# A graph-attention layer on one core: the fill work between attention steps is cut into smaller pieces

## The chip, the cores and the metric

The kernel runs on one core of a Trainium2 chip. The metric is the device time of one execution in microseconds (us). TensorE (PE), VectorE (DVE), ScalarE (ACT), GpSimd (POOL) and SyncE (SP) have instruction streams of their own [...].

## The reference

Eight frames `f` of 2048 nodes with 256 channels go through one masked attention layer with eight heads of 32 channels, a two-layer network, and three layer norms:

```python
qkv = jnp.einsum('fnc,ck->fnk', x, w_qkv)            # x: 8 x 2048 x 256
scores = jnp.einsum('fnhd,fmhd->fhnm', q, k) / sqrt(32)
scores = jnp.where(adj > 0, scores, -1e9)            # adj: 2048 x 2048, sparse
attn = softmax(scores, axis=-1)
t = jnp.einsum('fhnm,fmhd->fnhd', attn, v)
a = layernorm(x + t, ln1_g, ln1_b)
h = relu(a @ w1 + b1)
b = layernorm(a + h @ w2 + b2, ln2_g, ln2_b)
out = layernorm(x + b)
```

## The kernel before, in words

**Items.** The attention is a list of 1024 items `(f, qc, g, mb)`: frame, block of 512 query rows, group of four heads, block of 128 key rows. Sixteen items (`mb` 0 to 15) make a group, two groups make a block `(f, qc)`, four blocks make a frame. For one item:

- `scores` (L168): four matmuls (L176) write four heads of transposed scores into two PSUM pairs (of three, `ps_s`, used in turn). DVE adds the mask while it moves each pair to a tile `p` in SBUF (L179, two instructions), and ACT takes the exponential of the whole tile in place (L181). `p` has ten buffers.
- `values` (L185): four matmuls (L193) add `v` times `p` into a PSUM bank that the group owns for its sixteen items. After the last, ACT copies it to `oT` (L197).
- `add_up` (L205): the softmax denominators need the sum of the sixteen `p` tiles. Six items of `POOLED` are added to the group's first tile by GpSimd (L212). Items of the two `MOVED` chains are added to the chain's first tile by an accumulating DMA, which GpSimd issues (L209). The last item is left alone.

The main loop (L358) writes the order out by hand. At step `t` it calls `advance(t, banks)`, then `scores` of item `t + 2`, then `values` and `add_up` of item `t`. Each engine executes its part of that order.

**Fill work.** Everything else is a Python generator in the list `fill`, and `advance` emits pieces of it between items. A generator yields `k` when it is to go on `k` items later, `BANK` when its next piece needs a PSUM bank, and `TURNED` when it needs the tile `turned`, which one generator at a time may hold. `advance` hands out one bank in a step (two in odd steps of the "hurried" stretches: the last group of `qc` 3 and the first half group of a frame). All these banks are one and the same PSUM tile: of the two `ps_x` tiles one belongs to the running group and the other is for fill work, with one buffer. The generators are:

- `denominator` (L237), four items after each group: sixteen matmuls of the four remaining `p` tiles with a matrix of ones (L245) as one piece, an ACT copy (L247), four transposes (L252), the reciprocal (L257).
- `tail` (L263), one for each block, two items after the denominators of its second group: transposes of `oT` (L272), the scaling by the reciprocals (L273), the residual `x` added by an accumulating DMA (L277), `norm`, two transposes into `turned` (L287), two GpSimd operations over 128x1024 (L290, L291), the two layers (L297, L307), `norm`, two more GpSimd operations (L312, L313), the second residual (L314), `norm`, and the store (L317).
- `norm` (L215): for each of four row blocks bn_stats and bn_aggr on DVE (L219, L220), two row blocks to a step; four small GpSimd operations (L224 to L228); two items later four ACT scalings (L231) in one step.
- `project` (L127), four in a frame for the next frame: transposes, then `kT`, `qT` and `v` in six pieces with one bank each (L150, L159) and an ACT copy each.
- `mask_ahead`, in frame 0 alone: turns the adjacency matrix into the mask tiles.

New denominators and tails go to the front of `fill`, the rest to its end.

Of the kernel before, what the change touches and what calls it, by code (L numbers as in the profile page):

```python
# [18 lines left out]
P = 128  # L19
H = 8  # L20
D = 32
CH = 512
# [3 lines left out]

SUM_MIN = 1e-25
SUM_MAX = 1e19
BANK, TURNED = -1, -2

MASKED = -57344.0

# [21 lines left out]
def fast_path(ctx, tc, cst, x, adj, out, RS):  # L54
    nc = tc.nc
    F, N, C = x.shape
    NCK, TPC, MB = N // CH, CH // P, N // P
# [16 lines left out]
    ctx.enter_context(tc.manual_schedule())  # L74

    ident, identb, wqkv, w1s, w2s = cst["ident"], cst["identb"], cst["wqkv"], cst["w1s"], cst["w2s"]
    state = {"pair": 0, "side": None, "turn": 0, "turned": False}

    def score_pair():
        i = state["pair"]  # L80
# [85 lines left out]
    PT, O, OT, RC = {}, {}, {}, {}  # L166
# [16 lines left out]
    LAST = MB - 1  # L183
# [14 lines left out]

    POOLED = (0, 3, 5, 8, 10, 12, 14)
    MOVED = ((1, 4, 7, 11), (2, 6, 9, 13))
    SUM = 4

    def add_up(item):  # L205
# [9 lines left out]
    def norm(t):  # L215
        mv = small.tile([P, TPC, nc.vector.BN_AGGR_DIM], F32, name="mv")
        for j in range(TPC):
            st = small.tile([P, nc.vector.BN_STATS_DIM], F32, name="st")
            nc.vector.bn_stats(st, t[:, j, :])  # L219
            nc.vector.bn_aggr(mv[:, j, :], st)  # L220
            if j % 2:
                yield 1
        rs = small.tile([P, TPC], F32, name="rs")
        nc.gpsimd.tensor_scalar(rs, mv[:, :, 1], EPS, 1.0, op0=ALU.add, op1=ALU.mult)  # L224
        nc.gpsimd.tensor_tensor(rs, rs, cst["mhalf"], ALU.pow)  # L225
        nb = small.tile([P, TPC], F32, name="nb")
        nc.gpsimd.tensor_tensor(nb, mv[:, :, 0], rs, ALU.mult)  # L227
        nc.gpsimd.tensor_scalar(nb, nb, -1.0, 1.0, op0=ALU.mult, op1=ALU.mult)  # L228
        yield 2
        for j in range(TPC):  # L230
            nc.scalar.activation(t[:, j, :], t[:, j, :], AF.Identity, bias=nb[:, j:j + 1], scale=rs[:, j:j + 1])  # L231
        yield 1

    def rows(v):
        return v[:, None, :].to_broadcast([P, TPC, C])

    def denominator(f, qc, g):  # L237
        grp = (f, qc, g)
        terms = [PT.pop((f, qc, g, LAST))] + [PT.pop((f, qc, g, chain[0])) for chain in MOVED + (POOLED,)]
        yield BANK  # L240
        ps = bank()
        for n, term in enumerate(terms):
            for h in range(4):
                r = D * h
                nc.tensor.matmul(ps[r:r + D, :], cst["ones"], term[:, h, :], start=(n == 0), stop=(n == 3))  # L245
        dT = op.tile([P, CH], F32, name="dT")
        nc.scalar.copy(dT, ps)  # L247
        yield 1
        yield BANK
        ps = bank()  # L250
        for j in range(TPC):
            nc.tensor.transpose(ps[:, j * P:(j + 1) * P], dT[:, j * P:(j + 1) * P], ident)  # L252
        if g == 0:
            RC[f, qc] = op.tile([P, TPC, H], F32, name="rc")
        rc = RC[f, qc]
        den = ps.rearrange("p (j c) -> p j c", c=P)[:, :, ::D]
        nc.vector.reciprocal(rc[:, :, 4 * g:4 * g + 4], den)  # L257
        nc.vector.tensor_tensor(RS[:, 0], RS[:, 0], den, ALU.add)
        nc.vector.tensor_tensor(RS[:, 1], RS[:, 1], den, ALU.min)
        if g == 1:  # L260
            start(items.index((f, qc, g, LAST)) + SUM + 2, tail(f, qc), urgent=True)

    def tail(f, qc):  # L263
        rc = RC.pop((f, qc))
        xin = x[f, qc * CH:(qc + 1) * CH, :].rearrange("(j p) c -> p j c", p=P)
        y = yp.tile([P, TPC, C], F32, name="y")
        for gg in range(2):
            oT = OT.pop((f, qc, gg))
            yield BANK
            ps = bank()  # L270
            for j in range(TPC):
                nc.tensor.transpose(ps[:, j * P:(j + 1) * P], oT[:, j * P:(j + 1) * P], ident)  # L272
            nc.vector.tensor_tensor(y[:, :, gg * P:(gg + 1) * P].rearrange("p j (h d) -> p j h d", d=D),  # L273
                                    ps.rearrange("p (j h d) -> p j h d", h=4, d=D),
                                    rc[:, :, 4 * gg:4 * gg + 4, None].to_broadcast([P, TPC, 4, D]), ALU.mult)
        yield 1
        nc.gpsimd.dma_start(y, xin, accum_op=ALU.add)  # L277
        yield 5
        yield from norm(y)
        yield TURNED  # L280
        state["turned"] = True
        yT = work.tile([P, 2, CH], F32, name="turned")
        for a in range(2):
            yield BANK
            ps = bank()
            for j in range(TPC):
                nc.tensor.transpose(ps[:, j * P:(j + 1) * P], y[:, j, a * P:(a + 1) * P], ident)  # L287
            nc.scalar.activation(yT[:, a, :], ps, AF.Identity, bias=cst["be1c"][:, a:a + 1], scale=cst["g1c"][:, a:a + 1])  # L288
        yield 1
        nc.gpsimd.tensor_tensor(y, y, rows(cst["g1r"]), ALU.mult)  # L290
        nc.gpsimd.tensor_tensor(y, y, rows(cst["be1b2r"]), ALU.add)  # L291
        hT = work.tile([P, 2, CH], F32, name="hT")
        for d in range(2):
            yield BANK
            ps = bank()
            for a in range(2):
                nc.tensor.matmul(ps, w1s[:, a, d * P:(d + 1) * P], yT[:, a, :], start=(a == 0), stop=(a == 1))  # L297
            nc.scalar.activation(hT[:, d, :], ps, AF.Relu, bias=cst["b1s"][:, d:d + 1], scale=1.0)  # L298
        state["turned"] = False
        yield 1  # L300
        z = y
        for jj in range(0, TPC, 2):
            yield BANK
            ps = bank()
            for j in range(jj, jj + 2):
                for d in range(2):
                    nc.tensor.matmul(ps[:, (j - jj) * C:(j - jj + 1) * C], hT[:, d, j * P:(j + 1) * P], w2s[:, d, :],  # L307
                                     start=(d == 0), stop=(d == 1))
            nc.vector.tensor_tensor(z[:, jj:jj + 2, :], ps.rearrange("p (b c) -> p b c", c=C), z[:, jj:jj + 2, :], ALU.add)  # L309
        yield 1  # L310
        yield from norm(z)
        nc.gpsimd.tensor_tensor(z, z, rows(cst["g2r"]), ALU.mult)  # L312
        nc.gpsimd.tensor_tensor(z, z, rows(cst["be2r"]), ALU.add)  # L313
        nc.gpsimd.dma_start(z, xin, accum_op=ALU.add)  # L314
        yield 7
        yield from norm(z)
        nc.sync.dma_start(out[f, qc * CH:(qc + 1) * CH, :].rearrange("(j p) c -> p j c", p=P), z)  # L317


    fill = []  # L320

    def start(t, gen, urgent=False):
        fill.insert(0 if urgent else len(fill), [t, gen, 1])

    def advance(t, banks):
        for e in list(fill):
            while e[0] <= t:
                if e[2] == BANK:  # L330
                    if not banks:
                        break
                    banks -= 1
                elif e[2] == TURNED and state["turned"]:
                    break
                e[2] = next(e[1], None)
                if e[2] is None:
                    fill.remove(e)
                    break
                if e[2] > 0:  # L340
                    e[0] = t + e[2]
# [5 lines left out]
    items = [(f, qc, g, mb) for f in range(F) for qc in range(NCK) for g in range(2) for mb in range(MB)]  # L347
# [10 lines left out]
    for t, (f, qc, g, mb) in enumerate(items):  # L358
        if mb == 0 and t:
            state["side"] = 1 - state["side"]  # L360
        if f == 0 and g == 0 and mb == 0 and qc + 1 < NCK:
            start(t, mask_ahead(qc + 1))
        if g == 1 and mb == 0 and (f or qc == NCK - 1) and (f + 1 < F or qc + 1 < NCK):
            load_mask(f + (qc + 1) // NCK, (qc + 1) % NCK)

        if f + 1 < F and (qc, g, mb) in AHEAD:
            start(t, project(f + 1, AHEAD.index((qc, g, mb))))
        if mb:
            hurry = (g, qc) == (1, NCK - 1) or (f and g == qc == 0 and mb < MB // 2)
            advance(t, 2 if hurry and mb % 2 else 1)  # L370
        if t + LEAD < len(items):
            nf, _, ng, nmb = items[t + LEAD]
            t0 = t
            while (nf, nmb // TPC, 1) not in V:
                advance(t0, 1)
                t0 += 1
            scores(items[t + LEAD])
        values(items[t])
        add_up(items[t])
        if mb == LAST:  # L380
            start(t + SUM, denominator(f, qc, g), urgent=True)
    t = len(items)
    while fill:
        t += 1
        advance(t, 1)
# [236 lines left out]
```

## Time and profile before

| | before |
|---|---|
| time, median of 3 | 4048.52 us (4035.02 to 4049.99) |
| span of the profiled execution | 4037.3 us |
| PE busy | 3291.4 us, 82% |
| DVE busy | 2732.3 us, 68% |
| POOL busy | 2621.6 us, 65% |
| ACT busy | 2440.2 us, 60% |
| granted TensorE clock | 0.961 |

The busy shares are means over stretches with different limits: items with no fill work, items with a matmul piece ahead of them, items with norm work. The chain that ended last, which the page lists, covers only the end of the program from 3989.90 us on. To see the limits, the timeline has to be read item by item; the start of each group of eight L176 records (two records to each of four matmuls) marks an item.

### The profile page before, as it was taken

How to read it: one execution, taken by the hardware profiler on the slowest of the kernel's cores; microseconds unless marked ns; L12 is line 12 of the kernel's file. 1: busy time of each engine (PE TensorE's matmuls, PEld its weight loads, DVE VectorE, ACT ScalarE, POOL GpSimd, SP SyncE). 2: the span in 40 equal slices, each digit the busy share in tenths (PEclk: the TensorE clock that was granted, in tenths of full speed). 3: DMA queues.
4: the chain of work that ended last, by engine and by line, in shares of the span. 5: the costliest groups of instructions: out<-in, count | busy, mean ns of one | idle time of the engine just before them, and what ended most of it. 6: DMA issues, size and time to landing. Idle time of an engine off the chain costs nothing. (4 is left out here: it accounts for less than half of the span.)

```text
span 4037.3 us, 53723 instructions
## 1 busy us (share of the span) xinstructions
PE 3291.4 (82%) x22020; PEld 1044.4 (26%) x22020; DVE 2732.3 (68%) x3175; ACT 2440.2 (60%) x1953; POOL 2621.6 (65%) x1355
## 2 busy tenths in 40 slices
PE   7776988888888888888888887888878888888883
PEld 4221332222322223222222222222222222322221
DVE  3766746777477765777667775687756877477772
ACT  4655655666466654666656665566655666566662
POOL 1565656767467765776657766577656777477774
PEclk9988999999999999999999999999999999999996
DMA  4666646667366654677556656476555677367662
GB/s 141 156 142 140 148 95 128 139 145 152 68 146 148 140 128 81 145 148 151 122 112 133 140 126 145 101 153 144 115 128 114 143 148 155 73 141 146 135 137 58
DMA packets 138797, 525.60 MB, mean 130 GB/s; under 512 B 10160, under 2 KB 76848, under 8 KB 85296
## 3 DMA queue, kind: packets, MB, share of 16 engines
q0 software_dynamic: 89088, 436.24, 54.7%
q1 hardware_dynamic: 47104, 83.89, 6.0%
q8 instruction: 174, 2.85, 0.3%
q10 hardware_dynamic: 2352, 1.97, 0.2%
q14 instruction: 79, 0.65, 0.0%
HBM read 98.44 MB, written 20.97 MB: 30 GB/s over the span
## 5 line engine op out<-in xcount | busy, mean ns | idle before, releaser
L179 DVE TENSOR_TENSOR p<-s,mask 128x1024 f32<-128x1024 f32 x2048 | 2410.4, 1219 | 1083.8 <-PE s L176 902.5
L181 ACT ACTIVATE p<-p 128x2048 f32<-128x2048 f32 x1024 | 1952.3, 1910 | 1353.1 <-DVE p L179 1061.1
L212 POOL TENSOR_TENSOR p<-p 128x2048 f32<-128x2048 f32 x384 | 1790.3, 4663 | 931.2 <-ACT p L181 912.3
L176 PE MATMUL s<-qT,kT 32*128 32x512 f32 x8192 | 1212.2, 662 | 354.4 <-DVE p L179 353.5
L193 PE MATMUL x<-p,v 128*32 128x512 f32 x8192 | 1118.1, 618 | 21.4 <-ACT p L181 21.2
L176 PEld LDWEIGHTS s<-qT,kT 32*128 32x128 f32 x8192 | 329.7, 188 | 1010.9 <-DVE p L179 879.4
L209 POOL DMA_DIRECT2D p<-p x384 | 371.8, 979 | 145.7 <-ACT p L181 101.8
L193 PEld LDWEIGHTS x<-p,v 128*32 128x32 f32 x8192 | 162.9, 109 | 834.8 <-issue 528.3
L150 PE MATMUL x<-turned,wqkv 128*128 128x512 f32 x480 | 244.5, 634 | 75.9 <-ACT kT L152 44.2
L245 PE MATMUL x<-p,ones 128*32 128x512 f32 x2048 | 236.3, 602 | 18.9 <-DMA p<-p 8.9
L231 ACT ACTIVATE y<-y,nb,rs 128x256 f32<-128x256 f32 x384 | 197.8, 585 | 40.4 <-POOL nb L228 40.4
L219 DVE BATCH_NORM_STATS2 st<-y 128x6 f32<-128x256 f32 x384 | 155.9, 406 | 23.3 <-DMA y<-in_x_dram 23.3
L297 PE MATMUL x<-turned,w1s 128*128 128x512 f32 x256 | 130.4, 633 | 31.2 <-ACT turned L288 27.1
L159 PE MATMUL x<-wqkv,turned 128*128 128x128 f32 x896 | 124.9, 297 | 34.1 <-ACT qT L152 20.2
L150 PEld LDWEIGHTS x<-turned,wqkv 128*128 128x128 f32 x480 | 84.4, 194 | 239.5 <-issue 94.4
L312 POOL TENSOR_TENSOR y<-y,g2r 128x1024 f32<-128x1024 f32 x32 | 78.1, 2442 | 101.8 <-ACT y L231 101.8
L159 PEld LDWEIGHTS x<-wqkv,turned 128*128 128x128 f32 x896 | 113.5, 206 | 77.2 <-ACT qT L152 38.6
L307 PE MATMUL x<-w2s,hT 128*128 128x256 f32 x512 | 127.6, 392 | 4.0 <-ACT oT L197 1.5
L290 POOL TENSOR_TENSOR y<-y,g1r 128x1024 f32<-128x1024 f32 x32 | 75.7, 2367 | 60.0 <-issue 57.3
L245 PEld LDWEIGHTS x<-p,ones 128*32 128x32 f32 x2048 | 64.0, 111 | 186.2 <-issue 137.2
L307 PEld LDWEIGHTS x<-w2s,hT 128*128 128x128 f32 x512 | 92.0, 189 | 68.8 <-issue 33.3
L287 PE MATMUL x<-ident,y 128*128 128x128 f32 x256 | 53.9, 318 | 62.5 <-ACT y L231 24.4
(67 smaller groups left out, 1366.4 us busy)
## 6 DMA issues: line engine op xcount, KB each, us to landing
p<-p POOLq DMA_DIRECT2D x384, 1024.0 KB, 8.8
y<-in_x_dram POOLq DMA_DIRECT2D x64, 512.0 KB, 6.6
mask<-md SPq DMA_DIRECT2D x28, 1024.0 KB, 14.2
in<-in_x_dram SPq DMA_DIRECT2D x32, 512.0 KB, 13.1
in<-in_adj_dram SPq DMA_DIRECT2D x32, 512.0 KB, 6.4
out_dram<-y SPq DMA_DIRECT2D x32, 512.0 KB, 9.1
md<-mask SPq DMA_DIRECT2D x4, 1024.0 KB, 6.4
wqkv<-in_L_gnn_w_qkv_dram ACTq DMA_DIRECT2D x1, 768.0 KB, 5.9
```

The costliest lines, as they stand in the source:

```text
L150: nc.tensor.matmul(ps, wqkv[:, a, k0 + g * P:k0 + (g + 1) * P], xT[:, a, :], start=(a == 0), stop=(a == 1))
L159: nc.tensor.matmul(ps[:, j * P:(j + 1) * P], xT[:, a, j * P:(j + 1) * P], wqkv[:, a, 2 * C + g * P:2 * C + (g + 1) * P], start=(a == 0), s ...
L176: nc.tensor.matmul(ps2[half][:, j, :], KT[f, mb // TPC, g][r:r + D, (mb % TPC) * P:(mb % TPC + 1) * P], QT[f, qc][r:r + D, g, :], start=Tr ...
L179: nc.vector.tensor_tensor(pt[:, 2 * half:2 * half + 2, :], ps, MK[f, qc][:, mb, None, :].to_broadcast([P, 2, CH]), ALU.add)
L181: nc.scalar.activation(pt, pt, AF.Exp, scale=1.0 / math.sqrt(D))
L193: nc.tensor.matmul(O[grp][r:r + D, :], V[f, mb // TPC, g][:, mb % TPC, r:r + D], PT[item][:, h, :], start=(mb == 0), stop=(mb == LAST))
L209: nc.gpsimd.dma_start(PT[f, qc, g, chain[0]], PT.pop(item), accum_op=ALU.add)
L212: nc.gpsimd.tensor_tensor(first, first, PT.pop(item), ALU.add)
L219: nc.vector.bn_stats(st, t[:, j, :])
L231: nc.scalar.activation(t[:, j, :], t[:, j, :], AF.Identity, bias=nb[:, j:j + 1], scale=rs[:, j:j + 1])
L245: nc.tensor.matmul(ps[r:r + D, :], cst["ones"], term[:, h, :], start=(n == 0), stop=(n == 3))
L307: nc.tensor.matmul(ps[:, (j - jj) * C:(j - jj + 1) * C], hT[:, d, j * P:(j + 1) * P], w2s[:, d, :], start=(d == 0), stop=(d == 1))
```

## The change

It cuts the fill work finer and changes its order.

- `norm` takes one row block to a step in the statistics and in the ACT scalings. Two pairs of GpSimd operations in `tail` are put in separate steps, and so is the issue of the second residual DMA.
- `POOLED` and `MOVED` are laid out anew over the group; the item left alone is 14 and no longer the last.
- The products with ones are emitted in two halves, each after a `BANK`; both write the same bank.
- In `tail` the rows of a block are dealt to the partitions as `(p j)` in place of `(j p)`, so that each partition's four rows are 4 KB in one piece in memory. The transposes of `dT` and `oT` then take every fourth column.
- `fill` is sorted by rank: denominators, then tails, then the rest, each by age. At most two tails run at a time (`ROOM`).

```diff
-    POOLED = (0, 3, 5, 8, 10, 12, 14)
-    MOVED = ((1, 4, 7, 11), (2, 6, 9, 13))
+    POOLED = (0, 3, 6, 8, 11, 13, 15)
+    MOVED = ((1, 4, 7, 10), (2, 5, 9, 12))
+    ALONE = 14
...
             nc.vector.bn_aggr(mv[:, j, :], st)
-            if j % 2:
-                yield 1
+            yield 1
...
             nc.scalar.activation(t[:, j, :], t[:, j, :], AF.Identity, bias=nb[:, j:j + 1], scale=rs[:, j:j + 1])
-        yield 1
+            yield 1
...
         for n, term in enumerate(terms):
+            if n == 2:
+                yield BANK
             for h in range(4):
...
-            nc.tensor.transpose(ps[:, j * P:(j + 1) * P], dT[:, j * P:(j + 1) * P], ident)
+            nc.tensor.transpose(ps[:, j * P:(j + 1) * P], dT[:, j::TPC], ident)
...
-            start(items.index((f, qc, g, LAST)) + SUM + 2, tail(f, qc), urgent=True)
+            start(items.index((f, qc, g, LAST)) + SUM + 2, tail(f, qc), 1)
...
     def tail(f, qc):
+        yield ROOM
+        state["tails"] += 1
...
-        xin = x[f, qc * CH:(qc + 1) * CH, :].rearrange("(j p) c -> p j c", p=P)
+        xin = x[f, qc * CH:(qc + 1) * CH, :].rearrange("(p j) c -> p j c", p=P)
...
-                nc.tensor.transpose(ps[:, j * P:(j + 1) * P], oT[:, j * P:(j + 1) * P], ident)
+                nc.tensor.transpose(ps[:, j * P:(j + 1) * P], oT[:, j::TPC], ident)
...
         nc.gpsimd.tensor_tensor(y, y, rows(cst["g1r"]), ALU.mult)
+        yield 1
         nc.gpsimd.tensor_tensor(y, y, rows(cst["be1b2r"]), ALU.add)
...
         nc.gpsimd.tensor_tensor(z, z, rows(cst["g2r"]), ALU.mult)
+        yield 1
         nc.gpsimd.tensor_tensor(z, z, rows(cst["be2r"]), ALU.add)
+        yield 1
         nc.gpsimd.dma_start(z, xin, accum_op=ALU.add)
...
-    def start(t, gen, urgent=False):
-        fill.insert(0 if urgent else len(fill), [t, gen, 1])
+    def start(t, gen, rank=2):
+        fill.append([t, gen, 1, rank])
+        fill.sort(key=lambda e: e[3])
...
-                elif e[2] == TURNED and state["turned"]:
+                elif e[2] == TURNED and state["turned"] or e[2] == ROOM and state["tails"] == 2:
                     break
...
-            start(t + SUM, denominator(f, qc, g), urgent=True)
+            start(t + SUM, denominator(f, qc, g), 0)
```

More of the change, by code (lines that the diff above doesn't have):

```diff
@@ L28 @@
 SUM_MAX = 1e19
-BANK, TURNED = -1, -2
+BANK, TURNED, ROOM = -1, -2, -3
 MASKED = -57344.0
@@ L76, in fast_path @@
     ident, identb, wqkv, w1s, w2s = cst["ident"], cst["identb"], cst["wqkv"], cst["w1s"], cst["w2s"]
-    state = {"pair": 0, "side": None, "turn": 0, "turned": False}
+    state = {"pair": 0, "side": None, "turn": 0, "turned": False, "tails": 0}
     def score_pair():
@@ L238, in denominator @@
         grp = (f, qc, g)
-        terms = [PT.pop((f, qc, g, LAST))] + [PT.pop((f, qc, g, chain[0])) for chain in MOVED + (POOLED,)]
+        terms = [PT.pop((f, qc, g, ALONE))] + [PT.pop((f, qc, g, chain[0])) for chain in MOVED + (POOLED,)]
         yield BANK
@@ L316, in tail @@
         yield from norm(z)
-        nc.sync.dma_start(out[f, qc * CH:(qc + 1) * CH, :].rearrange("(j p) c -> p j c", p=P), z)
+        nc.sync.dma_start(out[f, qc * CH:(qc + 1) * CH, :].rearrange("(p j) c -> p j c", p=P), z)
+        state["tails"] -= 1
     fill = []
-    def start(t, gen, urgent=False):
-        fill.insert(0 if urgent else len(fill), [t, gen, 1])
+    def start(t, gen, rank=2):
+        fill.append([t, gen, 1, rank])
+        fill.sort(key=lambda e: e[3])
     def advance(t, banks):
```

## The prediction

> **What bounds the kernel now.** I read the page's costliest groups first, then four windows of one frame, then the timeline item by item. The groups give the work of one item:
>
> ```profile
> L179 DVE TENSOR_TENSOR p<-s,mask 128x1024 f32<-128x1024 f32 x2048 | 2410.4, 1219 | 1083.8 <-PE s L176 902.5
> L181 ACT ACTIVATE p<-p 128x2048 f32<-128x2048 f32 x1024 | 1952.3, 1910 | 1353.1 <-DVE p L179 1061.1
> L212 POOL TENSOR_TENSOR p<-p 128x2048 f32<-128x2048 f32 x384 | 1790.3, 4663 | 931.2 <-ACT p L181 912.3
> L176 PE MATMUL s<-qT,kT 32*128 32x512 f32 x8192 | 1212.2, 662 | 354.4 <-DVE p L179 353.5
> L193 PE MATMUL x<-p,v 128*32 128x512 f32 x8192 | 1118.1, 618 | 21.4 <-ACT p L181 21.2
> ```
>
> For 1024 items that is DVE 2.36 us an item, PE 1.18 + 1.09 = 2.27 us, ACT 1.91 us. No engine is the limit throughout: DVE waits longest for PE, PE for DVE, ACT for DVE. The windows are the four query blocks of frame 3, 32 items each (PE, PEld, DVE, ACT, POOL busy, clock, DMA share, GB/s):
>
> ```profile
> 1567.70:1691.93 124.23, 102.84 (x678) 31.79 (x677) 84.29 (x99) 74.64 (x60) 74.90 (x40) 0.96 0.53 111
> 1691.93:1798.01 106.08, 88.20 (x625) 23.98 (x625) 83.99 (x99) 71.17 (x53) 83.16 (x43) 0.98 0.73 154
> 1798.01:1913.20 115.19, 100.05 (x683) 31.39 (x683) 84.09 (x99) 75.51 (x61) 82.20 (x42) 0.99 0.67 141
> 1913.20:2052.20 139.00, 115.34 (x744) 40.03 (x744) 84.23 (x99) 79.53 (x68) 87.16 (x46) 0.98 0.57 123
> ```
>
> The reader is to see that DVE's 84 us is the same in each, that PE's work grows with the projections, and that PE still idles 15 to 24 us in a block: 78 us in the frame's 484.5. So the time is neither PE's sum nor DVE's, but the sum over items of whichever was longer in each. The timeline shows the kinds of item. First a plain one:
>
> ```profile
> 1742.91 1.14 PE L176 MATMUL s<-qT,kT 32*128 32x512 f32 x8 [0.41 <-DVE p L179]
> ...
> 1743.98 1.07 PE L193 MATMUL x<-p,v 128*32 128x512 f32 x8
> ...
> 1744.19 2.35 DVE L179 TENSOR_TENSOR p<-s,mask 128x1024 f32<-128x1024 f32 x2 [0.20 <-PE s L176]
> ```
>
> The next item begins at 1745.47, so it took 2.56 us: DVE's 2.35 plus a handover of 0.2. PE idles 0.41. Next the products with ones, then an ACT bunch, then two bank pieces in one step:
>
> ```profile
> 1704.39 3.62 PE L245 MATMUL x<-p,ones 128*32 128x512 f32 x32
> ...
> 1707.94 1.14 PE L176 MATMUL s<-qT,kT 32*128 32x512 f32 x8
> ...
> 1709.25 2.36 DVE L179 TENSOR_TENSOR p<-s,mask 128x1024 f32<-128x1024 f32 x2 [3.19 <-PE s L176]
> ```
>
> ```profile
> 1752.54 2.06 ACT L231 ACTIVATE y<-y,nb,rs 128x256 f32<-128x256 f32 x4
> ...
> 1754.91 1.14 PE L176 MATMUL s<-qT,kT 32*128 32x512 f32 x8
> ...
> 1756.17 2.36 DVE L179 TENSOR_TENSOR p<-s,mask 128x1024 f32<-128x1024 f32 x2 [2.54 <-PE s L176]
> ```
>
> ```profile
> 2029.80 1.98 PE L150 MATMUL x<-turned,wqkv 128*128 128x512 f32 x4
> ...
> 2033.24 0.57 ACT L152 COPY kT<-x 128x512 f32<-128x512 f32 x1
> ...
> 2033.86 1.98 PE L150 MATMUL x<-turned,wqkv 128*128 128x512 f32 x4 [2.07 <-ACT kT L152]
> ```
>
> While PE works on a piece, the scores wait behind it and DVE idles 3.19 us. In the last pair PE waits 2.07 us for the bank, because the copy stands behind an exponential on ACT; that item took 8.08 us, one with a single such piece 3.98.
>
> **What the Trainium skill says.** "TensorE: Matmul & The Clock Gate", section "Architectural detail: the array is 16× 32×32, not 1× 128×128", calls ACT and DVE strict FIFO. The trace agrees: the 0.57 us copy waits its turn and PE with it. "SBUF — State Buffer", section "Door 1: The DMA port swizzle", says SBUF lines are 16 bytes and that every access crossing to a new line pays; the transposes with every fourth f32 column would do so. No row before shows such a read. "DMA: Bandwidth & Descriptors", section "SWDGE vs HWDGE vs iDMA", has GpSimd's cores compute a descriptor pair for each operation. The trace agrees: issuing 1 MB in 8 KB rows (L209) occupied POOL 979 ns, 512 KB in 1 KB rows 1632 (L277) and 1341 ns (L314).
>
> **The change part by part.** I take item times from starts of successive L176 groups, and find where each piece goes by counting yields through `advance`. A norm grows from 5 steps to 10, three norms in a tail by 15, the GpSimd steps add 3: a tail of 38 to 41 items becomes 55. Tails start every 32, so two overlap, the third never meets `ROOM`, and one tail's norm work lies beside another's matmul pieces. No projection ends late for its frame by this count. Per frame:
>
> (a) Statistics. Twelve norms make 24 pair-steps; one costs about 0.8 us where nothing hides it (3.36 against 2.55): 19 us. After, 48 single steps; DVE has 2.36 + 0.58 = 2.94 us, 0.38 above a plain item. About a third lie beside a PE piece (3.98 us, DVE slack 1.6) and are free: 32 x 0.38 = 12. Gain 7.
>
> (b) ACT bunches. The four scalings (2.06 us) delay an exponential or a bank copy. In block 1 they and the transposes behind them made items of 4.10 and 5.34, where 2.55 and about 3.3 (ACT 1.91 + 0.76 + 0.59) suffice: 3.6. Block 0 has 5.93 for 3.4: 2.5. Block 2 has 5.52 and 4.56 for 4.0 and 4.05: 2. Block 3 has 8.98 and 10.08 for 4.0 and 8.5: 6.6. Gain 14.7. One scaling a step gives ACT 2.5 us, under the plain item.
>
> (c) Two halves of ones. A whole product took 5.50 and a plain item beside it 2.55, together 8.05; two halves take 2 x (2.14 + 1.85) = 7.98. Nothing by itself; the hiding is counted in (a). The second half needs no copy in between. The old order put ten pairs of other bank pieces in one step per frame, the new one eight; a pair costs 8.1 + 2.55 against 2 x 3.98, 2.7 more. Two fewer is 5.4; I take 3, since some new pairs carry scalings.
>
> (d) Splitting L290 and L291 leaves an item between the last `turned` transposes and L297, which waited for their copy: 5.62 against 4.05 in block 1. Gain 1.6; the second split and the later DMA issue are hidden behind other tails' work.
>
> Sum 26 us, checked by pricing every item of block 1 anew: 32 x 2.55 = 81.6, four halves +5.8, L297 and L307 +6.0, transposes +1.7, statistics +3.8, the rest +1.2, together 100.1 against 106.08. I take 25 for each of six frames; frame 7 has no projections, 20; frame 0 is held by mask work, 12. Gain 182.
>
> (e) GpSimd. The same six additions and six issues; 64 issues may fall from 1.5 to 1.0 us (estimate from L209's row count), 32 us off its total. But the items around 6 to 13 of a block's first group go faster: some 21 us for additions 4 x 4.66, four chain issues 3.7, L312 and L313 4.8 and two residual issues 2: 29. It falls 8 us behind and holds p buffers and DMA issues. Behind the queued addition stand the issues and the norm's small operations, for which ACT's scaling waits. Ten blocks without projections there, at nothing to 8 us each; I take 2.5: +25. In ones, item 15's addition now precedes the second half by five items, over 13 us, against 4.66: hidden.
>
> (f) Strided transposes. 512 loads now at 141 ns: at nothing to double (+72 us, all on the path). These items have PE slack; I take +10.
>
> (g) The drain, 81 us after the last L193. Two tails are now unfinished, and the last addition (4.66) comes before the denominators; faster transfers give back some 2. +6, from 0 to +20.
>
> Together 4048 - 182 + 25 + 10 + 6 = 3907; I say 3905.
>
> **Rivals.** GpSimd limits (0.13): all 8 us in all blocks outside hurried ones, some 24: 192 in place of 25, about 4070 with the rest; half of it some 3980. For it: 29 us of work in 21. Against: POOL's chain waits mostly for ACT (912.3 us), so it has room. I name 4000. Work merely moved (0.05): single steps at full price 0.58 and nothing hidden gives 28 in (a), 16 us a frame lost: 3905 + 8 x 16 = 4033, no change. Slower (0.08): strided loads on the path (+62 more), drain +14, and (a) and (b) failing (+160): 4140. For it: the longer tails keep `turned` and the fill bank contended. A larger gain (0.10): nothing late on GpSimd, pairs of banks cheaper, loads free: 3905 - 35 - 40 = 3830.
>
> **How the numbers follow.** The forecast has 0.64. Faster by over 0.5% takes it, the larger gain and most of the GpSimd case: 0.86; within 0.5%: 0.06; slower: 0.08. The range 3800 to 4025 spans the larger gain and the GpSimd case at its likely size.
>
> **What would show it.** Right: L231 and L219 in ones, PE idle down by some 130 us at unchanged busy time, the L179 wait for L176 down from 902.5. Frame 3 near 460 us. Wrong: DVE waiting for DMA or POOL in L179, ACT L231 waiting for POOL, PEld L252 and L272 well over 142 ns, or PE busy growing.

## The result and the profile after

| | before | after |
|---|---|---|
| time, median of 4 | 4043.27 us (4035.02 to 4049.99) | 3927.93 us (3923.38 to 3929.01) |
| ratio | 1 | 0.9714, 95% interval 0.969 to 0.9737 |
| PE busy | 3291.4 us | 3282.7 us |
| DVE's wait for scores (L179 for L176) | 902.5 us | 726.9 us |
| DVE's wait for a chain transfer (L179 for p) | 30.1 us | 59.4 us |
| frame 3 (128 items) | 484.5 us | 471.15 us |
| from the start of the last item's scores to the end | 88.2 us | 77.3 us |

The change made the kernel 2.9% faster; 3905 was forecast. The groups of the page of after (out, in, count, busy, mean ns, idle before and its cause; line numbers have moved: the GpSimd addition, L212 before, is L213 now, and L210 issues a chain transfer, the accumulating DMA of a `MOVED` item):

```profile
L179 DVE TENSOR_TENSOR p<-s,mask 128x1024 f32<-128x1024 f32 x2048 | 2409.3, 1218 | 989.9 <-PE s L176 726.9
L181 ACT ACTIVATE p<-p 128x2048 f32<-128x2048 f32 x1024 | 1956.8, 1911 | 1273.8 <-DVE p L179 1017.5
L213 POOL TENSOR_TENSOR p<-p 128x2048 f32<-128x2048 f32 x384 | 1815.9, 4730 | 790.1 <-ACT p L181 788.3
L176 PE MATMUL s<-qT,kT 32*128 32x512 f32 x8192 | 1202.8, 657 | 302.6 <-DVE p L179 302.5
L193 PE MATMUL x<-p,v 128*32 128x512 f32 x8192 | 1120.4, 620 | 2.9 <-ACT p L181 2.9
```

The work is the same; the idle time in front of it is shorter. DVE waits 175.6 us less for scores, but its whole idle time before L179 fell by only 93.9 us (1083.8 to 989.9): part came back as waits for something else, 29 us of it for chain transfers. The four blocks of frame 3, in the same columns as those of before:

```profile
1529.73:1648.58 118.85, 102.59 (x690) 33.27 (x689) 84.83 (x102) 74.58 (x59) 79.66 (x42) 0.99 0.57 118
1648.58:1755.13 106.55, 88.84 (x625) 24.84 (x625) 83.95 (x96) 72.36 (x55) 81.93 (x43) 0.95 0.74 159
1755.13:1864.14 109.01, 98.97 (x681) 31.61 (x681) 84.14 (x98) 75.27 (x61) 81.21 (x42) 1.00 0.66 142
1864.14:2000.88 136.74, 115.11 (x730) 39.93 (x729) 83.45 (x97) 79.62 (x69) 80.97 (x42) 0.95 0.56 124
```

Against 124.23, 106.08, 115.19 and 139.00 before, three blocks won 5.4, 6.2 and 2.3 us, and the second, the one without projections, won nothing: 106.55, where 100.1 was forecast. Its timeline shows two halves of the ones product in neighbouring items, as intended:

```profile
1661.66 1.90 PE L247 MATMUL x<-p,ones 128*32 128x512 f32 x16
...
1663.49 1.14 PE L176 MATMUL s<-qT,kT 32*128 32x512 f32 x8
...
1665.44 1.90 PE L247 MATMUL x<-p,ones 128*32 128x512 f32 x16
...
1667.27 1.14 PE L176 MATMUL s<-qT,kT 32*128 32x512 f32 x8
```

One such item takes 1667.27 - 1663.49 = 3.78 us. Further on the same timeline shows where the block's gain went (L317 and L319 are the two GpSimd operations behind the second norm, L321 issues the second residual):

```profile
1679.65 1.91 ACT L181 ACTIVATE p<-p 128x2048 f32<-128x2048 f32 x1 [0.40 <-DVE p L179]
...
1686.81 2.63 POOL L319 TENSOR_TENSOR y<-y,be2r 128x1024 f32<-128x1024 f32 x1
1689.12 1.15 POOL L210 DMA_DIRECT2D p<-p  x1
1689.74 1.42 POOL L321 DMA_DIRECT2D y<-in_x_dram  x1
1690.27 1.77 POOL L210 DMA_DIRECT2D p<-p  x1
1690.83 5.79 POOL L213 TENSOR_TENSOR p<-p 128x2048 f32<-128x2048 f32 x1
...
1697.56 2.36 DVE L179 TENSOR_TENSOR p<-s,mask 128x1024 f32<-128x1024 f32 x2 [1.89 <-DMA p<-p]
1698.00 0.86 POOL L210 DMA_DIRECT2D p<-p  x1 [1.38 <-DMA p<-p]
...
1704.95 2.36 DVE L179 TENSOR_TENSOR p<-s,mask 128x1024 f32<-128x1024 f32 x2 [4.48 <-DMA p<-p]
```

The first L210 here is the chain transfer of item 9. Its exponential, the first line, ended at 1681.56 (1679.65 + 1.91), but GpSimd's queue came to it only 7.6 us later; in the same block of before this was 2.1 us. It and the transfer of item 10 then left within 1.2 us of each other with the residual between them. The median from issue to landing of L210 is 8.6 us; the first of these took 8.3 us, the second 14.6, from 1690.27 to 1704.83. A `p` tile comes free only when its transfer has landed: both L179 above began 0.12 us after a landing (1697.44 and 1704.83). So DVE waited 1.89 + 4.48 = 6.4 us for a place to write. Both waits recur in the second block of frames 2 to 7, at about the same size; in frame 1 they are smaller (0.7 and 2.3 us).

A second cost goes with this stall. In the windows of these microseconds (columns as above) PE's granted clock is halved for 10 us, from the time of the second wait on:

```profile
1690.00:1700.20 10.20, 6.44 (x52) 1.41 (x48) 8.25 (x11) 5.71 (x4) 8.82 (x6) 1.00 0.98 180
1700.30:1710.40 10.10, 5.45 (x28) 1.00 (x24) 4.47 (x5) 4.08 (x3) 7.63 (x2) 0.50 0.88 182
```

In that time the matmuls take nearly twice as long, these eight score records 2.09 us in place of 1.14, and their item 3.88 in place of 2.55:

```profile
1706.23 2.09 PE L176 MATMUL s<-qT,kT 32*128 32x512 f32 x8 [4.65 <-DVE p L179]
```

The half clock lasts 10.2 us in this block in each of frames 3 to 7. That the idle PE is what brings it on is not shown.

### The profile page after: what moved, and what is told of

Read it like the earlier page. It is cut to its first block, busy times and chain, and to the rows that moved or that the text cites. A ratio compares the mean times of both kernels' runs of the same rounds, so it can differ in the third digit from the quotient of the medians.

```text
span 3926.0 us, 53576 instructions
## 1 busy us (share of the span) xinstructions
PE 3282.7 (84%) x22020; PEld 1056.5 (27%) x22020; DVE 2732.5 (70%) x3175; ACT 2446.9 (62%) x1953; POOL 2593.9 (66%) x1355
## 5 line engine op out<-in xcount | busy, mean ns | idle before, releaser
L179 DVE TENSOR_TENSOR p<-s,mask 128x1024 f32<-128x1024 f32 x2048 | 2409.3, 1218 | 989.9 <-PE s L176 726.9
L213 POOL TENSOR_TENSOR p<-p 128x2048 f32<-128x2048 f32 x384 | 1815.9, 4730 | 790.1 <-ACT p L181 788.3
L176 PE MATMUL s<-qT,kT 32*128 32x512 f32 x8192 | 1202.8, 657 | 302.6 <-DVE p L179 302.5
L176 PEld LDWEIGHTS s<-qT,kT 32*128 32x128 f32 x8192 | 328.1, 187 | 957.9 <-DVE p L179 801.3
L210 POOL DMA_DIRECT2D p<-p x384 | 381.9, 1010 | 285.0 <-ACT p L181 205.8
L231 ACT ACTIVATE y<-y,nb,rs 128x256 f32<-128x256 f32 x384 | 223.5, 587 | 39.8 <-POOL nb L228 39.7
L302 PE MATMUL x<-turned,w1s 128*128 128x512 f32 x256 | 139.8, 672 | 29.7 <-ACT hT L303 24.6
L317 POOL TENSOR_TENSOR y<-y,g2r 128x1024 f32<-128x1024 f32 x32 | 80.5, 2516 | 51.6 <-DVE p L179 26.6
L224 POOL TENSOR_SCALAR rs<-mv 128x4 f32<-128x4 f32 x96 | 18.4, 192 | 135.5 <-DVE mv L221 131.1
L225 POOL TENSOR_TENSOR rs<-rs,mhalf 128x4 f32<-128x4 f32 x96 | 99.3, 1035 | 8.0
```

The lines of the kernel that those rows point to most:

```text
L176: nc.tensor.matmul(ps2[half][:, j, :], KT[f, mb // TPC, g][r:r + D, (mb % TPC) * P:(mb % TPC + 1) * P], QT[f, qc][r:r + D, g, :], start=Tr ...
L179: nc.vector.tensor_tensor(pt[:, 2 * half:2 * half + 2, :], ps, MK[f, qc][:, mb, None, :].to_broadcast([P, 2, CH]), ALU.add)
L210: nc.gpsimd.dma_start(PT[f, qc, g, chain[0]], PT.pop(item), accum_op=ALU.add)
L213: nc.gpsimd.tensor_tensor(first, first, PT.pop(item), ALU.add)
```

## The experiments

Each ratio is to the kernel before, with its 95% interval; after is 0.9714. First, parts of the change undone in the kernel after.

**The statistics in pairs again:**

```diff
             nc.vector.bn_aggr(mv[:, j, :], st)
-            yield 1
+            if j % 2:
+                yield 1
```

> The kernel after, with the statistics of two row blocks in one step again; the ACT scalings stay one to a step. My theory: single statistics hide beside PE pieces, 7 us a frame by term (a), so about 3975 us (+50). Rival theory, that only the ACT bunches mattered: within 10 us of 3928. If item 15 of the blocks with the second GpSimd backlog changes place, +-20 on top of either.

3942.58 us, ratio 0.9738 (0.9716 to 0.976). The loss of 15 us (10 by the ratios, whose intervals overlap) is at the edge of what these runs tell apart, and far from the 50 expected; it is nearer to the rival theory. The single statistics are worth little in this kernel. With the pairs DVE's wait for `p` is 31.5 us in place of 59.4, so some 28 us of what the single ones save may come back as that wait.

**The four scalings in one step again:**

```diff
             nc.scalar.activation(t[:, j, :], ..., bias=nb[:, j:j + 1], scale=rs[:, j:j + 1])
-            yield 1
+        yield 1
```

> The kernel after, with the four ACT scalings in one step again; the statistics stay one to a step. My theory: the bunches delay exponentials and bank copies, 14.7 us a frame by term (b), so about 4010 us (+80 to +100). Rival theory, that the statistics carried the gain: within 15 us of 3928.

4001.0 us, ratio 0.9888 (0.9872 to 0.9905): 73 us lost, a little under the expected 80. The bunches were the dearer half of the norm.

**Both:**

> The kernel after, with both parts of the norm in their old steps. My theory: the norm carries nearly all the gain, so 4020 to 4060 us, no better than before apart from the drain's 11 us. Rival theory, that halves, order and layout carry it: under 3970.

4030.39 us, ratio 0.9966 (0.9953 to 0.9978). Without the two parts of the norm the rest of the change brings 0.3%, and 8.7 us of that lie behind the last item's scores (79.5 us in place of 88.2). The norm is worth 102 us in the kernel after.

**The ones product in one piece:**

```diff
         for n, term in enumerate(terms):
-            if n == 2:
-                yield BANK
```

> The kernel after, with the sixteen products with ones as one piece again. My theory: splitting gains nothing by itself, only the statistics beside the second half, one or two a group at 0.3 us; so 3930 to 3950. Rival theory, that the long piece starves DVE: 64 groups at about 1.5 us or more, over 4020.

3949.74 us, ratio 0.9761 (0.9745 to 0.9778): 22 us lost, at the upper end of what was expected and far from the rival's 90. Before, a whole piece and a plain item took 5.50 + 2.55 = 8.05 us; two halves take 2 x 3.78 = 7.56. That is 0.5 us a group and 31 us in 64 groups, of the measured size. But this account is not shown: in frame 3's second block the first nine items take 27.29 us with the whole product and 27.24 with the halves, and of the 26 us between the two profiled executions 10 lie in frame 0. Whether the halves gain by themselves or by the statistics beside the second one, as expected, stays open.

**The old layout of additions and chains:**

```diff
-    POOLED = (0, 3, 6, 8, 11, 13, 15)
-    MOVED = ((1, 4, 7, 10), (2, 5, 9, 12))
-    ALONE = 14
+    POOLED = (0, 3, 5, 8, 10, 12, 14)
+    MOVED = ((1, 4, 7, 11), (2, 6, 9, 13))
+    ALONE = 15
```

> The kernel after, with the old items in the GpSimd additions and in the two DMA chains (item 15 left alone again). My theory: the drain waits again for the last chain transfer of item 13, +11 us; inside the frames the change is within 2 us a block either way, since the work is the same; so 3930 to 3965. Rival theory, that the old places crowd GpSimd in the new order of tails: two more stalls a block of 3 us or more, over 4050.

3891.91 us, ratio 0.9606 (0.9585 to 0.9628): faster than the change as made, by 36 us, against both theories. The span behind the last item's scores is 77.8 us, so the expected 11 us there were not lost either. The second block fell from 106 or 107 to about 103 us and frame 7 from 434.9 to 424.4. The timeline of this kernel's same stretch:

```profile
1676.88 1.15 POOL L210 DMA_DIRECT2D p<-p  x1
1677.49 1.44 POOL L321 DMA_DIRECT2D y<-in_x_dram  x1
1678.05 5.47 POOL L213 TENSOR_TENSOR p<-p 128x2048 f32<-128x2048 f32 x1
...
1682.54 1.81 POOL L210 DMA_DIRECT2D p<-p  x1
...
1685.22 2.36 DVE L179 TENSOR_TENSOR p<-s,mask 128x1024 f32<-128x1024 f32 x2 [1.80 <-DMA p<-p]
...
1692.88 2.36 DVE L179 TENSOR_TENSOR p<-s,mask 128x1024 f32<-128x1024 f32 x2 [2.07 <-ACT p L181]
```

GpSimd is as late as in the kernel after (item 9's transfer leaves 7.6 us after its exponential), but item 10 is an addition, so the next chain transfer, item 11's, leaves 5.7 us behind item 9's and takes 10.2 us. The wait of 1.8 us stays and that of 4.48 shrinks to 2.07 (the profile names ACT, but this L179 too began 0.12 us after a landing, that of item 11's transfer at 1692.76). The half clock of PE shrinks from 10.2 to 3.4 us. Hence the new layout put the transfers of items 9 and 10 side by side where the queue runs late.

**The rows dealt as before:**

```diff
-        xin = x[f, qc * CH:(qc + 1) * CH, :].rearrange("(p j) c -> p j c", p=P)
+        xin = x[f, qc * CH:(qc + 1) * CH, :].rearrange("(j p) c -> p j c", p=P)
...
-                nc.tensor.transpose(ps[:, j * P:(j + 1) * P], oT[:, j::TPC], ident)
+                nc.tensor.transpose(ps[:, j * P:(j + 1) * P], oT[:, j * P:(j + 1) * P], ident)
```

The store and the transposes of `dT` are changed in the same way.

> The kernel after, with rows dealt (j p) again: 1 KB pieces, contiguous columns in the transposes of dT and oT. My theory: the strided weight loads cost 68 ns each (210 against 142) but lie in items with PE slack, some 0.3 us in each of 128 pieces at most 35 us; the longer issues (about 0.5 us each, 64 of them) lengthen the GpSimd backlog; together within 20 us of 3928. Rival theory, that long rows carry the gain: over 3960.

3930.82 us, ratio 0.9699 (0.9681 to 0.9716): no difference from the change. The long rows shorten the issues on GpSimd (L281 1023 ns in place of 1486, L321 1192 in place of 1637) and lengthen the weight loads (below). Both were undone together, so it is not shown whether neither is on a path or the two offset each other.

Next, GpSimd's lateness as the cause of the wait. Two kernels put work out of its way by lengthening the pauses, five items before the first of the two GpSimd operations (`x_late`), or before the transfer alone (`x_dmalate`):

```diff
+        yield 5
         nc.gpsimd.tensor_tensor(z, z, rows(cst["g2r"]), ALU.mult)
```

```diff
-        yield 1
+        yield 6
         nc.gpsimd.dma_start(z, xin, accum_op=ALU.add)
```

> The kernel after, with the two 128x1024 GpSimd operations after the second norm and the second residual transfer each put five items later (a pause of 5 before the first of them). My theory: GpSimd has 29 us of work in items 6 to 13 of the plain blocks and issues the transfer of item 9 some 8 us late, so that DVE waits 6.4 us for a p buffer at items 15 and 16; with the three taken out of that stretch the waits go, 7 us in each of 8 blocks, so 3865 to 3890 us and DVE's wait for p transfers down from 59.4 to under 20 us. Rival theory, that the chain's three-item spacing is too short for an 8.6 us transfer whatever GpSimd does: the waits stay, within 10 us of 3928.

> The kernel after, with only the second residual transfer put five items later; the two GpSimd operations stay. If the waits at items 15 and 16 come from the operations on GpSimd's queue: most of them stay, 3910 to 3930. If they come from the transfers' collision (the one of item 10 took 12.8 us from issue's end to landing beside the residual): they shrink by half or more, 3890 to 3905.

4098.03 us (ratio 1.0108, 1.0083 to 1.0134) and 4052.92 us (1.0016, 1.0003 to 1.003): both far slower than the kernel after, against every forecast. Their totals say nothing on the question, for a second cause came in. The waits for `p` fell from 59.4 to 2.5 us in the first and to 7.5 in the second, but the scaling L277 now waited (wait totals of that line in the first, us and times):

```profile
its engine sat idle before it (us, times) until:
  DMA out_dram<-y: 195.3, 29
```

A tail five items longer stores its rows so late that the tail after the next, which takes over its `y` buffer, has to wait: 195.3 us in 29 waits, and 146.7 us in 15 in the second kernel. So a tail of some 55 items, started every 32 with two buffers, was already near its limit.

**The same shift at an unchanged length,** three items later, taken back from the pause behind the transfer:

```diff
+        yield 3
         nc.gpsimd.tensor_tensor(z, z, rows(cst["g2r"]), ALU.mult)
...
         nc.gpsimd.dma_start(z, xin, accum_op=ALU.add)
-        yield 7
+        yield 4
```

> The kernel after, with the two 128x1024 operations after the second norm and the second residual transfer three items later, and the pause behind that transfer cut from 7 to 4, so that the tail ends where it ended and the y buffers come free as before; the longer tails of the two runs with a 5-item delay lost 195 and 147 us to a wait of L277 for the store, so they could not decide. My theory, GpSimd's backlog in items 6 to 13 of the plain blocks: the two waits at items 15 and 16 there (6.4 us) shrink to under 3, about 3890 to 3905 us. Rival theory, the chain transfers of items 9 and 10 standing next to each other in the new layout: the waits stay, 3920 to 3935.

3917.73 us, ratio 0.9693 (0.9673 to 0.9714), no clear gain and not the time expected. The waits for `p` did go, from 59.4 to 9.4 us in all. But the second block kept 105 us, because the residual transfer now had four items to land and GpSimd still came late to it: the chain transfer just ahead of it, item 12's, left 6.4 us after its exponential. DVE waits at the statistics, and its work on the scores behind them is held up:

```profile
1690.09 1.44 POOL L322 DMA_DIRECT2D y<-in_x_dram  x1
...
1700.19 0.43 DVE L220 BATCH_NORM_STATS2 st<-y 128x6 f32<-128x256 f32 x1 [2.97 <-DMA y<-in_x_dram]
```

The rival's prediction, that the waits stay where they are, failed: items 9 and 10 still leave next to each other, 2.5 us apart, but with no residual between them, and the second lands after 12.5 us without a wait. What stays is the lateness; it shows in another place.

**The shift with the old layout:**

> The same shift of the GpSimd operations together with the old item layout of sums and chains. If both causes are at work, the second block of a frame comes down from 103 us (old layout alone) to about 100 and the time to 3865 to 3885 us; if the layout had been the whole cause: 3885 to 3895, no different from the old layout alone (3892).

3888.13 us, ratio 0.9623 (0.96 to 0.9645), not to be told from the old layout alone (0.9606), as the second forecast had it. The second block is 102.0 us, not the 100 of the first.

**GpSimd's work itself taken away.** The pauses stay, the two operations go, so the second norm's scale and shift are left out:

```diff
-        nc.gpsimd.tensor_tensor(z, z, rows(cst["g2r"]), ALU.mult)
         yield 1
-        nc.gpsimd.tensor_tensor(z, z, rows(cst["be2r"]), ALU.add)
```

> The kernel after without the two 128x1024 GpSimd operations behind the second norm (scale and shift of the second norm are left out); every pause stays, so all other pieces keep their items. It takes 4.8 us of GpSimd work out of each tail. My theory, GpSimd's backlog of 8 us in items 6 to 13 of the plain blocks: the waits at items 15 and 16 there shrink from 6.4 to under 2 us and DVE's wait for p transfers from 59.4 to under 25, the second block of a frame to 101 or 102, the time to 3870 to 3890 us. Rival theory, that the two chain transfers issued next to each other delay one another whatever GpSimd has to do: the waits keep at least two thirds, 3905 to 3925 us.

3896.94 us, ratio 0.9646 (0.9629 to 0.9664), between the two forecasts. 6 of the 31 us lie behind the last item's scores (71.1 us), where the operations stood on the way to the end. In the second block of frame 3 the first wait is gone and the second is 2.5 us; the waits for `p` fell from 59.4 to 26.5 us in all, and the second blocks from 106 or 107 to 102 or 103. Item 9's transfer now leaves 1.9 us after its exponential, about as in the kernel before, so the backlog in front of these two is gone. Item 10's leaves 2.5 us behind it, again with the residual between, and still takes 14.9 us. So some 4 of the block's 6.4 us are GpSimd's backlog; the other 2.5 are the slow landing of item 10's transfer behind its two neighbours. The old layout, with the backlog but without the neighbour, also takes away only a part.

**The norm alone, in the kernel before:**

> The kernel before, with only the norm in single steps (statistics and scalings); all else as before. My theory: the norm is worth some 100 us of its own, as undoing it cost 102, less a part because a whole product with ones hides less; 3945 to 3975 us. Rival theory, that it pays only together with the new order of tails and the halves: over 4010.

3986.53 us, ratio 0.9862 (0.9842 to 0.9883), about half of what it is worth in the kernel after, and outside the forecast. Here the second block grew to 109 or 110 us, and DVE waited longer still for `p` (total us, times, longest):

```profile
DVE p L179 <- DMA p<-p: 103.1, 34, 4.8
```

Which of the other parts (order by age, halves, split GpSimd steps, layout) helps the norm to its full worth was not separated. The wait just shown tells where the missing half may lie: DVE waits 73 us longer for `p` than in the kernel before, in the kernel after only 29 longer, and the difference of 44 is close to the 49 us that are missing.

## Why the prediction was right, point by point

**Direction and mechanism.** The forecast said that PE and DVE each set the time in turn, and that fill pieces side by side would shorten it at equal work. Busy times stayed within 1% on PE and DVE. PE's idle time in frame 3 fell from 78 to 471.15 - 405.52 = 66 us, in the whole program by 103 us where some 130 were named; frame 3 took 471 us, not about 460. The signs named were there: L231 one to a step, L179's wait for L176 down. So were two of the signs of being wrong: DVE waits longer for DMA in L179, and the weight loads of the strided transposes take well over 142 ns. The forecast is right in direction and kind, and 28 us too large (143 us forecast, 115 measured); undone, the norm is worth 102 of the 115 us. The tails became as long as counted: most take 54 to 57 items, where 55 was forecast (the sum given for it, 38 to 41 and 18 more, makes 56 to 59).

**The gain in the frames.** 182 - 25 - 10 = 147 us was forecast after costs, of which the frames brought about 100 in the profiled executions, and the end 11. The terms were off by more than the sum, and that their errors offset each other in part is luck:

- Term (a), statistics: 7 us a frame forecast, 15 us for the whole program when undone. Term (b), bunches: 14.7 a frame, some 100 us in all, measured 73. Together 102 measured, where the two terms give over 140. Their prices do not explain the miss of (a): a pair costs 0.8 us as I read it, and a single one 0.28 in a plain item (2.83 against 2.55), less than the 0.38 I took. Part of what they save seems to come back as the wait for `p` (28 us, above), which I had priced in (e) alone; the rest is open.
- Term (c), the halves: nothing forecast, 22 us measured (19 by the ratios). I had priced a half item at 3.99 us, PE's sum; it takes 3.78. How much of the 22 us is statistics beside the second half, which I had counted in (a), is open. The pairs of bank pieces in (c) and term (d), 1.6 us a frame, were not tested alone.

**Term (e), named, and right in the sum rather than in the place.** The backlog of 8 us, from 29 us of work in 21, was found as forecast: item 9's transfer 7.6 us late. I took 2.5 us a block in ten blocks, 25 in all; the second block of frame 3 waited 6.4 us, and its likes in the other frames ended at 106 or 107 us as well. Over the whole program DVE's wait for `p` rose by 29 us. I had let the backlog hold `p` buffers but had not seen that the new chains issue two transfers in a row there, nor that the second of them, behind the first and the residual, takes 14.6 us. With the old layout, which I had given no price, the kernel is 36 us faster.

**Term (f), strided loads:** +10 us taken; with rows and loads undone together, no difference. The loads of `dT` and `oT` did become longer (210 and 209 ns in place of 141 and 142). The Trainium skill, "SBUF — State Buffer", section "Door 1: The DMA port swizzle", had a penalty for each new 16-byte line right in kind; where it counts a stride of 4 f32 as free, these loads, with just that stride, say otherwise. That PE's slack hides them is likely, but not shown apart from the shorter issues.

**Term (g), the drain:** +6 forecast, -11 measured. Why it is shorter was not isolated; neither the old layout (77.8 us) nor the norm undone (79.5) brings the old end back, and the norm alone in the kernel before already shortens it to 80.1.

**The rivals.** GpSimd did become the limit, but mainly in one block of four and for 6.4 us, not for all 8 in 24 blocks. The change did not merely move the work.

## What to carry to other kernels

Where two engines take turns as the limit, put each one's extra work into the items in which the other is the limit; it is the time of each item that counts, so price an item and not an engine. Smoothing two engines speeds up the stretches in which a third one, idle on average, has most to do: recount its work against the new time of that stretch, and keep transfers that free a buffer from leaving side by side, with others between them, behind its queue. A longer pipeline of fill work uses up the slack of its buffers; know how many steps remain before adding one.

## What the runs showed of the hardware

- An accumulating transfer of a `p` tile (1 MB) lands 8.6 us after its issue in the median of after. One issued 1.2 us after another, with a residual of 512 KB between, took 14.6 us, and 14.9 with 2.5 us between the two (GpSimd's two operations taken away); without the residual, 12.5 (the shift at an unchanged length).
- After DVE's wait for `p` in frame 3 the granted clock of PE was 0.50 for 10 us; eight records of the scores took 2.09 us in place of 1.14.
- Loading 128 f32 columns as weights takes 140 to 142 ns when they are contiguous and 209 or 210 ns when every fourth is taken, about half as much again (L276 and L254 of after; with the rows dealt as before, the transposes' mean falls from 313 and 310 to 287 and 286 ns).
- Two items with half a product with ones take 2 x 3.78 us, one with a whole and a plain one 5.50 + 2.55, although PE's modelled time for the halves is not smaller (2 x 1.90 against 3.62 us).
